# Third chunk of an attention layer: scores clipped in their PSUM bank, biases added from there

## The chip, the cores and the metric

The kernel runs on one core of a Trainium2 chip. The metric is the device time of one execution in microseconds (us). Engines: TensorE (PE; its weight loads are PEld), VectorE (DVE), ScalarE (ACT), GpSimd (POOL) and SyncE (SP), which here issues most DMA transfers. Each engine works through its own queue in order and waits on semaphores for the others. SBUF is the large on-chip memory; PSUM, in banks of 128 x 512 float32, is where TensorE puts its products.

## The reference

A chain of layers, each added to the residual stream x of shape 2 x 1024 x 256 (batch, sequence, features): an attention with ALiBi biases, a feed-forward network with ternary weights, a Mamba block and a gated feed-forward network that keeps two of each four activations. The change is in the attention: 16 heads of 128, and cut to what matters

```python
xn = layernorm(x)
q, k, v = xn @ Wq.T, xn @ Wk.T, xn @ Wv.T            # 16 heads x 128
s = q @ k.T / sqrt(128)                              # clipped to +-1024
s = s + slope[h] * arange(kv_len) + causal           # causal: -inf for later keys
x = x + softmax(s) @ v @ Wo.T
```

## The kernel before

**Chunks and heads.** The two sequences of 1024 rows are cut in two halves each, four chunks `CH[k] = (b, u)` of 512 queries. `attention()` goes through chunks and heads in order; per head it makes four query tiles `j` of 128 rows in `scores`. A tile's keys reach up to width `W = (u * 4 + j + 1) * 128`: in the chunks with `u = 0` (the first and the third, k = 0 and 2) W is 128, 256, 384 and 512, in the others 640 to 1024.

**One tile.** A score product (`s`, L362) goes into one of the two PSUM banks of tag "s". It is the negated score. DVE's clip (L366, scalar_tensor_tensor) takes the minimum with `CLIP` and the maximum with `lower`, a constant SBUF tile which is −1024 or, for masked keys, a huge number, and writes the SBUF tile `ss`. DVE's reduce (L372, tensor_tensor_reduce) adds the head's biases `alibi` from SBUF in place and accumulates the minimum `nm`; ACT's exponential (L377) uses `nm` as its bias and accumulates the row sum `rs`. Two tiles later (`LAG`) `turn` transposes the tile (`pt` on PE L293, copy `pT` L296), then `values` makes `z` (L304, copy `zs` L309), and `project` makes `o` (L318) and adds it to x, scaled by the reciprocal `rr` (L314, L324). The next head's `pq`, `pk` (L335) and `pv` (L342) are issued in the middle of a head.

**What runs beside it.** While chunk k's attention runs, `rest(k - 1)` brings the chunk before through its other three layers. A table of costs (`cost`) spreads these pieces between the attention's tiles. A tile scheduler orders each engine's instructions from modelled times when the program is built, and chooses the engine of every `nc.any` copy; so an edit of one place can move others. Beside the third chunk (k = 2) these stand, for the second chunk: the ternary FFN (`g_f`, `u_f` L441, `ssp` L491, `fo` L502), the Mamba block's projections (`in` L608, `dtl`, `bcp`), its scan, and the kept-two FFN.

**The scan.** The Mamba block has 512 channels in four blocks c of 128, and 16 states n. For every (c, n): SP's DMA fetches the rows `bs` and `cs`; POOL multiplies `db = du * bs` (L736); ACT makes `da = exp(dl * a)` into PSUM (L750); DVE scans `hs` (L757); POOL multiplies `hc = hs * cs` (L771); PE adds `hc` transposed into the bank `y` (L701). Each block needs `dl` and `du` first: `dt` (PE L547), four activations, `sr` (DVE L568, L569), `dl` (POOL L570, and DVE L572 beside the third chunk) and `du` (POOL L574). These steps of block c + 1 are issued at n = 8 of block c. `db` and `hs` have four buffers each, `hc` five, `cs` four and `bs` five. After a block's 16 states, `gate` copies `y` out, turns it back and multiplies it by the gate `sz` (L793).

**Banks.** PSUM has eight banks, shared by tags: "s" 2, "mm" 3 (turns, z, o, q, k, v), "y" 1, "r" 2 (FFN, Mamba, `da`).

Of the kernel before, what the change touches and what calls it, by code (L numbers as in the profile page):

```python
# [18 lines left out]
B, S, D = 2, 1024, 256  # L19
# [15 lines left out]
CLIP = 1024.0  # L35
# [6 lines left out]
def kernel(  # L42
# [190 lines left out]
    for h in range(H):  # L233
        nc.gpsimd.affine_select(
            out=slope, in_=slope, compare_op=ALU.not_equal, fill=-SLOPES[h], base=-h,
# [18 lines left out]
    lower = ac.tile([P, S], F32, name="lower")  # L254
    nc.gpsimd.memset(lower, -CLIP)
    nc.gpsimd.affine_select(
        out=lower[:, S - P :], in_=lower[:, S - P :], compare_op=ALU.is_ge,
# [97 lines left out]
    def scores(k, h, j, st):  # L355

        W = (CH[k][1] * UT + j + 1) * P
        s = a3.tile([P, S], F32, tag="s", name=f"ss_{k}_{h}_{j}", bufs=4)
        for k0 in range(0, W, 512):
            n = min(512, W - k0)  # L360
            sp = ps_s(f"s_{k}_{h}_{j}_{k0}")
            nc.tensor.matmul(  # L362
                sp[:, :n], lhsT=st["qT"][:, j * P : (j + 1) * P], rhs=st["kT"][:, k0 : k0 + n],
                start=True, stop=True,
            )
            nc.vector.scalar_tensor_tensor(  # L366
                s[:, k0 : k0 + n], sp[:, :n], CLIP, lower[:, S - W + k0 : S - W + k0 + n],
                op0=ALU.min, op1=ALU.max,
            )
        nm = a3.tile([P, 1], F32, tag="nm", name=f"nm_{k}_{h}_{j}")  # L370
        pace["front"] = tiles[-2] if len(tiles) >= 2 else None
        pace["tile"] = nc.vector.tensor_tensor_reduce(  # L372
            out=s[:, :W], in0=s[:, :W], in1=st["alibi"][:, :W], scale=1.0,
            scalar=3.0e38, op0=ALU.add, op1=ALU.min, accum_out=nm,
        )
        tiles.append(pace["tile"])
        nc.scalar.activation(  # L377
            s[:, :W], s[:, :W], AF.Exp, bias=nm, scale=-1.0, accum_out=st["rs"][:, j : j + 1]
        )
        return s  # L380

    def attention():
# [7 lines left out]
        for i, (k, h) in enumerate(heads):  # L390
# [8 lines left out]
            for j in range(UT):  # L399
                s = scores(k, h, j, st)  # L400
                later.append((LAG, lambda a=(k, h, j, s, st): turn(*a)))
                if j == UT - 1:
                    later.append((LAG, lambda a=(k, h, st): values(*a)))
                    later.append((LAG + 1, lambda a=(k, h, st): project(*a)))
                if j == UT - 1 and h == H - 1:
                    for _, f in later:
                        f()
                    later = []
                else:
                    now = [f for n, f in later if n == 0]  # L410
                    later = [(n - 1, f) for n, f in later if n]
                    for f in now:
                        f()
                if j == 1 and i + 1 < len(heads):
                    qkv(*heads[i + 1], live[0], xns[heads[i + 1][0]])
                if j == 0 and h == H - 1 and k + 1 < len(CH):

                    with tc.issue_after(tiles[-UT].ins) if k == 0 else nullcontext():
                        normed(k + 1)
                yield k  # L420
# [464 lines left out]
    def kept_two_ffn(k):  # L885

        b, u = CH[k]
        W = 2 * U
        with ExitStack() as gctx:
# [158 lines left out]
```

## Time and profile before

Three runs took 1833.47, 1836.29 and 1837.93 us.

| | us |
|---|---|
| median of the three runs | 1836.29 |
| profiled execution, span | 1836.9 |
| PE busy | 1718.3 (94%) |
| DVE busy | 1218.3 (66%) |
| ACT busy | 963.7 (52%) |
| POOL busy | 832.2 (45%) |

The profiled execution's own time is its span of 1836.9 us, 0.6 above the median: what is read in the trace is read against that span, and nothing to speak of lies around it. The third chunk's attention lies between about 733 and 1113 us of the span.

How to read the lines shown below: a group of instructions has its line of the code, engine and operation, the tile it writes and the tiles it reads, shapes and count, then busy time and the mean of one in ns, then the engine's idle time just before them and what ended it. A row of windows gives a stretch of the span and each engine's busy time with its number of instructions, then TensorE's granted clock (1.00 is full speed), the DMA engines' share and GB/s. A row of the order in time gives start, duration, engine, line and operation.

### The profile page before, as it was taken

What the parts mean: (1) busy time and instruction counts of PE and PEld (TensorE: products, weight loads), DVE (VectorE), ACT (ScalarE), POOL (GpSimd) and SP (SyncE); (2) the same over time, 40 slices, a digit from 0 to 9 for tenths busy, and PEclk for the clock granted to TensorE, in tenths of its full rate; (3) what the DMA queues carried; (4) which work ended last, traced back from release to release, by engine and by line L of the source; (5) the groups of instructions that cost most, each with busy time, mean ns of one, the idle gap of its engine ahead of it and who ended that gap; (6) DMA issues with size and microseconds to landing.
All of it is one profiled execution on the core that took longest, in us unless ns stands there. A gap on an engine that the chain in (4) does not pass through costs nothing. (4 is left out here: it accounts for less than half of the span.)

```text
span 1836.9 us, 24217 instructions
## 1 busy us (share of the span) xinstructions
PE 1718.3 (94%) x7956; PEld 1144.2 (62%) x7956; DVE 1218.3 (66%) x2349; ACT 963.7 (52%) x1789; POOL 832.2 (45%) x674
## 2 busy tenths in 40 slices
PE   7999999998999999998888999999999999998899
PEld 4666666555656557755555667756656565566895
DVE  5666555777785473458886565557788655667975
ACT  3444474656563553555554545566555446446742
POOL 3324032588892000419998000418898500035870
PEclk9999999999999999999999999999999999999999
DMA  6443512466662311337787324227665430212541
GB/s 201 128 142 128 193 46 88 149 203 204 216 202 91 103 52 48 125 109 232 245 247 224 116 71 141 82 67 228 226 214 184 142 115 26 75 53 86 178 136 57
DMA packets 178301, 255.99 MB, mean 139 GB/s; under 512 B 16240, under 2 KB 90992, under 8 KB 177152
## 3 DMA queue, kind: packets, MB, share of 16 engines
q1 hardware_dynamic: 176752, 241.61, 41.4%
q0 software_dynamic: 1152, 12.58, 1.9%
q8 instruction: 63, 1.03, 0.2%
q14 instruction: 62, 0.51, 0.1%
q10 hardware_dynamic: 272, 0.26, 0.0%
HBM read 232.04 MB, written 22.35 MB: 138 GB/s over the span
## 5 line engine op out<-in xcount | busy, mean ns | idle before, releaser
L771 POOL TENSOR_TENSOR hc<-hs,cs 128x512 f32<-128x512 f32 x256 | 362.1, 1428 | 10.8 <-DVE ss L366 3.1
L362 PE MATMUL s<-kT,qT 128*128 128x512 f32 (+3 forms) x768 | 302.7, 495 | 19.9 <-DVE ss L366 18.0
L377 ACT ACTIVATE ss<-ss,nm 128x128 f32<-128x128 f32 (+7 forms) x256 | 198.8, 776 | 183.5 <-DVE nm L372 174.1
L366 DVE SCALAR_TENSOR_TENSOR ss<-s,lower 128x512 f32<-128x512 f32 (+3 forms) x384 | 204.6, 549 | 121.0 <-PE s L362 119.4
L736 POOL TENSOR_TENSOR db<-du,bs 128x512 f32<-128x512 f32 x192 | 259.2, 1356 | 44.4 <-DVE hs L757 30.6
L304 PE MATMUL z<-pT,v 128*128 128x512 f32 (+3 forms) x768 | 264.5, 492 | 10.9 <-ACT pT L296 10.2
L372 DVE CUSTOM_DVE_ANT_0 ss<-ss,alibi 128x128 f32<-128x128 f32 (+7 forms) x256 | 241.3, 945 | 3.5
L750 ACT ACTIVATE da<-dl,a_neg 128x512 f32<-128x512 f32 x256 | 177.9, 698 | 115.6 <-DVE hs L757 90.6
L304 PEld LDWEIGHTS z<-pT,v 128*128 128x128 f32 x768 | 142.8, 190 | 145.1 <-issue 92.7
L296 ACT COPY pT<-pt 128x512 f32<-128x512 f32 (+3 forms) x321 | 145.4, 474 | 162.0 <-PE pt L293 160.4
L293 PE MATMUL pt<-ident,ss 128*128 128x128 f32 x1152 | 180.3, 279 | 32.1 <-DVE x L324 18.5
L293 PEld LDWEIGHTS pt<-ident,ss 128*128 128x128 f32 x1152 | 140.0, 142 | 94.7 <-DVE x L324 33.0
L362 PEld LDWEIGHTS s<-kT,qT 128*128 128x128 f32 x768 | 127.9, 193 | 84.1 <-issue 43.4
L757 DVE TENSOR_TENSOR_SCAN hs<-da,db 128x512 f32<-128x512 f32 x128 | 153.8, 1210 | 38.6 <-ACT da L750 20.8
L757 DVE TENSOR_TENSOR_SCAN hs<-da,carry,db 128x512 f32<-128x512 f32 x128 | 159.1, 1269 | 24.4 <-POOL hc L771 14.7
L324 DVE SCALAR_TENSOR_TENSOR x<-o,rr,x 128x256 f32<-128x256 f32 x256 | 108.9, 476 | 76.7 <-PE o L318 76.5
L701 PE MATMUL y<-ident,hc 128*128 128x128 f32 x1024 | 144.8, 279 | 8.4 <-POOL hc L771 8.4
L342 PEld LDWEIGHTS pv<-wv,xT_a 128*128 128x128 f32 x1024 | 124.4, 192 | 37.1 <-issue 25.3
L342 PE MATMUL pv<-wv,xT_a 128*128 128x128 f32 x1024 | 125.8, 275 | 5.5 <-ACT zs L309 3.4
L701 PEld LDWEIGHTS y<-ident,hc 128*128 128x128 f32 x1024 | 121.0, 145 | 14.3 <-POOL hc L771 11.9
L318 PE MATMUL o<-wo,zs 128*128 128x256 f32 x512 | 125.4, 386 | 4.1 <-ACT kT L338 3.0
L335 PE MATMUL pq<-xT_a,wq 128*128 128x512 f32 x256 | 122.7, 601 | 0.7 <-ACT xT_a L148 0.7
(204 smaller groups left out, 2468.7 us busy)
## 6 DMA issues: line engine op xcount, KB each, us to landing
cs<-bcd SPq DMA_DIRECT2D x256, 256.0 KB, 3.8
bs<-bcd SPq DMA_DIRECT2D x192, 256.0 KB, 4.3
alibi<-alibi_d SPq DMA_DIRECT2D x32, 512.0 KB, 4.2
wq<-in_wqT_dram SPq DMA_DIRECT2D x64, 128.0 KB, 3.5
wk<-in_wkT_dram SPq DMA_DIRECT2D x64, 128.0 KB, 3.1
wv<-in_wvT_dram SPq DMA_DIRECT2D x64, 128.0 KB, 2.8
wo<-in_woT_dram SPq DMA_DIRECT2D x64, 128.0 KB, 2.8
alibi<-alibi_d SPq DMA_DIRECT2D x32, 256.0 KB, 3.6
```

What stands on the lines that cost most here:

```text
L293: nc.tensor.transpose(tp[:, i, :], s[:, (kb0 + i) * P : (kb0 + i + 1) * P], ident)
L304: nc.tensor.matmul(zp[:, q0:], lhsT=st["v_all"][:, kb, :], rhs=st["pts"][kb // 4][:, kb % 4, q0:], start=(kb == 0), stop=(kb == last),)
L342: nc.tensor.matmul(vp[:, t, :], lhsT=xT[:, c, t * P : (t + 1) * P], rhs=st["v"][:, c, :], start=(c == 0), stop=(c == KC - 1),)
L362: nc.tensor.matmul(sp[:, :n], lhsT=st["qT"][:, j * P : (j + 1) * P], rhs=st["kT"][:, k0 : k0 + n], start=True, stop=True,)
L366: nc.vector.scalar_tensor_tensor(s[:, k0 : k0 + n], sp[:, :n], CLIP, lower[:, S - W + k0 : S - W + k0 + n], op0=ALU.min, op1=ALU.max,)
L372: pace["tile"] = nc.vector.tensor_tensor_reduce(out=s[:, :W], in0=s[:, :W], in1=st["alibi"][:, :W], scale=1.0, scalar=3.0e38, op0=ALU.add, ...
L377: nc.scalar.activation(s[:, :W], s[:, :W], AF.Exp, bias=nm, scale=-1.0, accum_out=st["rs"][:, j : j + 1])
L701: nc.tensor.matmul(yTs[c][:, t * P : (t + 1) * P], lhsT=h[:, t * P : (t + 1) * P], rhs=ident, is_transpose=True, start=start and t == 0, s ...
L736: nc.gpsimd.tensor_tensor(db[i], du, brow.pop(i), ALU.mult)
L750: nc.scalar.activation(da[i], parts[c][0], AF.Exp, scale=a_neg[:, c, n : n + 1])
L757: nc.vector.tensor_tensor_scan(out=hs[i], data0=da.pop(i), data1=db.pop(i), initial=0.0 if first else carry[:, n, c : c + 1], op0=ALU.mult ...
L771: nc.gpsimd.tensor_tensor(hc[i], hs.pop(i), crow.pop(i), ALU.mult)
```

## The change

In the third chunk, where the whole tile fits one bank, the clip writes its result back into the PSUM bank it reads, and the reduce takes its first input from that bank and writes `ss` in SBUF for the first time. In the other chunks nothing changes (in the first one `k` is 0). The bank is thus read by the reduce, where it was last read by the clip. In the changed program the clip has line L368, the reduce L374 and the exponential L379; all lines behind are two higher.

```diff
         W = (CH[k][1] * UT + j + 1) * P
+        in_bank = k and W <= 512
         s = a3.tile([P, S], F32, tag="s", name=f"ss_{k}_{h}_{j}", bufs=4)
...
+            clipped = sp[:, :n] if in_bank else s[:, k0 : k0 + n]
             nc.vector.scalar_tensor_tensor(
-                s[:, k0 : k0 + n], sp[:, :n], CLIP, lower[:, S - W + k0 : S - W + k0 + n],
+                clipped, sp[:, :n], CLIP, lower[:, S - W + k0 : S - W + k0 + n],
                 op0=ALU.min, op1=ALU.max,
             )
...
         pace["tile"] = nc.vector.tensor_tensor_reduce(
-            out=s[:, :W], in0=s[:, :W], in1=st["alibi"][:, :W], scale=1.0,
+            out=s[:, :W], in0=clipped if in_bank else s[:, :W], in1=st["alibi"][:, :W], scale=1.0,
             scalar=3.0e38, op0=ALU.add, op1=ALU.min, accum_out=nm,
         )
```

## The prediction

> **What bounds the kernel now.** I first read the busy rows of the page: TensorE (PE) is the busiest engine over the whole span, with GpSimd (POOL) at under half.
>
> ```profile
> PE 1718.3 (94%) x7956; PEld 1144.2 (62%) x7956; DVE 1218.3 (66%) x2349; ACT 963.7 (52%) x1789; POOL 832.2 (45%) x674
> ```
>
> The edit touches only the third chunk's attention, so the average says little. Second view: the busy time in four stretches, chosen by what runs beside that attention (second chunk's ternary FFN, its Mamba input projection, its scan, its kept-two FFN).
>
> ```profile
> core 0: us, PE busy (x) PEld busy (x) DVE busy (x) ACT busy (x) POOL busy (x), PEclk, DMA share, GB/s
> 733.00:781.00 48.00, 45.77 (x238) 34.73 (x238) 23.57 (x68) 26.04 (x54) 22.03 (x19) 1.00 0.37 124
> 781.00:831.00 50.00, 48.44 (x176) 26.15 (x175) 31.48 (x69) 29.76 (x56) 11.17 (x13) 1.00 0.36 117
> 841.00:999.00 158.00, 125.90 (x644) 90.06 (x643) 131.75 (x189) 84.77 (x174) 156.37 (x120) 0.94 0.78 238
> 1000.00:1113.00 113.00, 111.25 (x468) 72.87 (x467) 59.08 (x142) 50.92 (x98) 5.61 (x5) 1.00 0.31 102
> ```
>
> PE is the bound in three of them (97 to 98% busy, whole clock). In the scan stretch (841 to 999) it isn't: POOL is busy for 156.37 of 158 us. There POOL sets the end, and VectorE (DVE) and PE have time to spare. Third view: the groups by shape, first in the scan stretch and then in the stretch behind it, where POOL is nearly idle.
>
> ```profile
> L372 DVE CUSTOM_DVE_ANT_0 ss<-ss,alibi 128x384 f32<-128x384 f32 x7 | 8.5, 1207 | 0.0
> L372 DVE CUSTOM_DVE_ANT_0 ss<-ss,alibi 128x512 f32<-128x512 f32 x7 | 7.3, 1049 | 0.2
> L366 DVE SCALAR_TENSOR_TENSOR ss<-s,lower 128x512 f32<-128x512 f32 x6 | 4.0, 672 | 0.0
> L366 DVE SCALAR_TENSOR_TENSOR ss<-s,lower 128x384 f32<-128x384 f32 x6 | 3.2, 540 | 0.0
> ```
>
> ```profile
> L366 DVE SCALAR_TENSOR_TENSOR ss<-s,lower 128x512 f32<-128x512 f32 x5 | 3.4, 687 | 1.3 <-PE s L362 1.3
> L372 DVE CUSTOM_DVE_ANT_0 ss<-ss,alibi 128x512 f32<-128x512 f32 x4 | 2.8, 692 | 0.2
> L372 DVE CUSTOM_DVE_ANT_0 ss<-ss,alibi 128x384 f32<-128x384 f32 x5 | 2.8, 552 | 0.0
> ```
>
> The reduce (L372, two inputs in SBUF) goes from 552 to 1207 ns and from 692 to 1049 ns once POOL is busy; the clip (L366, one input in PSUM) doesn't stretch (687 and 672). Fourth view: the order in time of POOL and of DVE around one head, where the reduces of widths 256, 384 and 512 start at 883.14, 886.49 and 890.79.
>
> ```profile
> 883.40 1.45 POOL L736 TENSOR_TENSOR db<-du,bs 128x512 f32<-128x512 f32 x1
> 884.82 1.27 POOL L771 TENSOR_TENSOR hc<-hs,cs 128x512 f32<-128x512 f32 x1
> 887.28 1.58 POOL L771 TENSOR_TENSOR hc<-hs,cs 128x512 f32<-128x512 f32 x1
> 891.28 1.72 POOL L736 TENSOR_TENSOR db<-du,bs 128x512 f32<-128x512 f32 x1
> ```
>
> ```profile
> 883.14 0.59 DVE L372 CUSTOM_DVE_ANT_0 ss<-ss,alibi 128x256 f32<-128x256 f32 x1
> 886.49 1.24 DVE L372 CUSTOM_DVE_ANT_0 ss<-ss,alibi 128x384 f32<-128x384 f32 x1
> 890.79 1.07 DVE L372 CUSTOM_DVE_ANT_0 ss<-ss,alibi 128x512 f32<-128x512 f32 x1
> ```
>
> The POOL product that meets a reduce takes 1.45, 1.58 and 1.72 us, where others take 1.27: the two engines make each other wait. Beside a clip or a scan POOL stays at 1.27.
>
> **The change part by part.** Only the 64 tiles of the third chunk (16 heads, widths 128 to 512) change; no DMA and no arithmetic instruction is added. The profiled execution spans 1836.9 us, 0.6 above the median of the runs (1836.29), so I add changes to the median as they are.
>
> 1. *Collision of reduce and POOL product.* The reduce keeps one SBUF input (the biases) and so looks like the clip. Per head it costs POOL 0.06 (the width-128 tile: 1.32 against 1.26), 0.18, 0.32 and 0.45, together 1.01 us. Seven heads (27 tiles) lie in the scan stretch: 7.1 us. Assigned operation by operation in the trace it is 7.2. POOL runs without gaps there, so that is a gain on the path: **−7.2**. What collides besides (L569, L572, with two SBUF inputs, 2.2 us) stays. The reduce itself gets shorter too (25.5 us for 27 tiles there, 13.2 at the undisturbed durations), on an engine with time to spare: 0.
>
> 2. *Clip writes PSUM, reduce reads PSUM.* No row shows DVE writing PSUM. ScalarE does: its 128x512 exponential into PSUM (L750) takes 691 ns, the one into SBUF (L377) 724: by that the clip would even be 0.03 us shorter. From the other side, a second full pass over each width would be 0.53 us per 512 elements, 1.33 per head, 9.3 in the scan stretch, where DVE stands at 131.75 of 158 and loses 12.3 of stretched reduces. I take 0, by the nearest rows; even the dear end hides beside POOL. [...] Here the clip from PSUM (687) is no slower than the reduce from SBUF (692), so I price it at nothing.
>
> 3. *Bank held until the reduce is done.* The two "s" banks came free after the clip; now a score product waits for the reduce two tiles back. Behind it on PE's queue stand z, the next head's q, k, v and the turns. The rows for this wait were PEld s on L366 at 31.3 us and PE s on L366 at 18.0 in the whole kernel. Beside the ternary FFN, where PE is the bound and two heads run, I take two or three of eight tiles as waiting for one reduce more (0.29 to 0.69 us, its undisturbed durations, mean 0.49): **+1.0** (0.5 to 1.5; a longer hold can't bring a gain). In the other stretches the wait shows in the order of work, steps 4 to 6. [...]
>
> 4. *Order around the projection.* In the built order, ScalarE loads tables three more times around the last gates (1.283 us each by the L377 table-load row), and a score product and transposes come ahead of dtl on PE (about 1.5 us). So the first db is some 2.7 us late; but the POOL order in time shows waits of 1.19 and 0.70 us for bs at 835.5 and 838.7, which this swallows: **+1.0** (0 to 2.7).
>
> 5. *The dt step at the two channel-block borders.* This is the largest loss. In the new order the score product of head 6, tile 3 stands behind the y additions of hc 0 to 4 (block 1), and z, q, k, v and dt (block 2) stand behind it. Before, z started at 885.0, with hc 3 and 4 still to come. POOL ends hc 4 at T = 888.86. So PE now waits until T, then 0.86 (the score products), 7.6 (z, pq, pk, pv), 1.8 (o) and the rest to dt: dt ends at about T + 12.0, against T + 7.4 before. The activations and both sr behind dt took 3.6 us: dl can start at T + 15.6. POOL gets there after ten products of 1.27, at T + 12.7, and waits **+2.9**; before, dl started at 902.19 with no gap. The same at the next border (head 8): there POOL already waits 0.69 at 947.78, and by the same count it becomes **+2.2** more. The first border keeps its order.
>
> 6. *Ends.* The last block's y additions and heads 11 to 15 (slacks of 0.15 to 0.3 us used up): **+0.8**.
>
> 7. *Clock.* TensorE's clock drops to 0.50 for 3.4 us right after PE gaps (at 831.6, 858.9, 903.3, 923.8, 992.1). Step 5 makes two new gaps of about 2 us. One new drop at full load costs up to 1.7; none or two are possible: **+1.7** (0 to 3.4).
>
> Sum: −7.2 + 1.0 + 1.0 + 2.9 + 2.2 + 0.8 + 1.7 = +2.4, so 1836.3 + 2.4 = 1838.7; I say 1839.
>
> **The rivals.**
>
> *A, forecast: collision gone, its gain paid back at the dt borders.* With the small ends of 3, 4 and 7 it is −0.8, with the large ones +6.3: 1835.5 to 1842.5. For it: at both borders POOL has no slack. Against: the order is static, but where PE waits depends on when POOL finishes, and POOL now finishes sooner.
>
> *B, faster: the gain stays.* If dt's chain is shorter than I count (the z matmuls start before T), POOL gets to dl with nothing late: with the small ends of 3, 4 and 7 that is −7.2 + 0.5 + 0.8 = −5.9; without one of the five clock drops as well −7.6. So 1828.7 to 1830.4; I take 1829.5. It needs dt to end before T + 9. For it: POOL is at 99% in that stretch and every product is counted.
>
> *C, slower: PE falls five products behind.* hc has five buffers, a db and an hc take 2.5 us, so POOL can run 12.6 us ahead of the y additions. The stretch of PE without y additions behind the held score product is some 10 us by the rows. If a waiting score product and a slow clock take it beyond 12.6, POOL stops at hc at three heads (5, 7 and 9's z) for some 3 us each: +2.4 + 9 = +11.4, about 1848. Against it: 2.6 us are missing.
>
> *D: the change doesn't separate the engines,* as the write of ss and the biases are still in SBUF. Then the 7.2 stays lost while the reordering is paid: +9.6, 1846. Against it: the clip, with lower and ss in SBUF, doesn't collide.
>
> **How the numbers follow.** A 0.40, B 0.28, C 0.24, D 0.08. About 0.3% (5.5 us) is what a measurement here can tell from no change: faster means under 1830.8, slower over 1841.8. A gives 0.30 same, 0.07 slower, 0.03 faster; B 0.25 faster, 0.03 same; C 0.24 slower; D 0.07 slower, 0.01 same. Together faster 0.28, same 0.34, slower 0.38. The range takes in B with a further 1.2 us and C with a further 2: 1827.5 to 1850. A's own is 1835.5 to 1842.5.
>
> **What would show it.** Step 1: products L771 and L736 average about 1.28 in the scan stretch, and the reduces there fall to about 290, 420, 555 and 690 ns; if they stay at 1.0 to 1.2 us, D. Step 2: the clip stays at 687 ns for 512; near 1.2 us would be the dear end. Step 5: POOL waits of 2 to 3 us for sr at its second and third L570; none means B. Step 7: more 0.5 digits around these. C: idle time of L771 released by PE's y. The forecast is wrong if POOL's scan stretch shrinks by 7 us with nothing behind it, or grows.

## The result, and the profile after

The changed kernel takes 1848.88 us (median of 4 runs, 1846.68 to 1850.38), the kernel before 1837.11 in the runs beside it: a ratio of 1.006, with a 95% interval of 1.0043 to 1.0078. It is slower by some 11 us. Executions of one and the same program lie up to 16 us apart in the runs below, so the ratios with their intervals decide there, and a single trace only says where the time went.

The first two views are the busy row of the page and the same four stretches as before. The busy totals of DVE and POOL fell (1218.3 to 1206.8 and 832.2 to 823.4), and the span rose by 8.0 us, to 1844.9.

```profile
PE 1722.6 (93%) x7956; PEld 1146.4 (62%) x7956; DVE 1206.8 (65%) x2351; ACT 965.1 (52%) x1790; POOL 823.4 (45%) x674
```

```profile
733.00:781.00 48.00, 45.42 (x223) 34.19 (x222) 23.03 (x66) 26.84 (x56) 21.58 (x19) 0.96 0.36 120
781.00:831.00 50.00, 49.55 (x183) 26.92 (x181) 27.00 (x61) 27.83 (x48) 6.65 (x9) 1.00 0.30 102
841.00:999.00 158.00, 126.96 (x604) 88.32 (x603) 118.73 (x183) 83.51 (x171) 142.39 (x115) 0.89 0.73 231
1000.00:1113.00 113.00, 107.74 (x461) 70.11 (x460) 61.90 (x147) 52.34 (x101) 13.62 (x12) 1.00 0.34 109
```

In the scan stretch POOL is no longer back to back: busy 142.39 of 158 us, where it was 156.37. It did five operations fewer in the same time. TensorE's granted clock there fell from 0.94 to 0.89.

The groups by shape in the scan stretch (taken from 845 to 1010, as all of it is later) show that the change did what it says:

```profile
L773 POOL TENSOR_TENSOR hc<-hs,cs 128x512 f32<-128x512 f32 x58 | 74.6, 1290 | 2.6 <-PE y L703 1.8 <-DMA cs<-bcd 0.9
L738 POOL TENSOR_TENSOR db<-du,bs 128x512 f32<-128x512 f32 x56 | 71.3, 1275 | 11.9 <-DMA cs<-bcd 4.6 <-DVE hs L759 4.5 <-DMA bs<-bcd 2.8
L368 DVE SCALAR_TENSOR_TENSOR s<-s,lower 128x512 f32<-128x512 f32 x7 | 4.9, 693 | 4.1 <-PE s L363 3.9
L374 DVE CUSTOM_DVE_ANT_0 ss<-s,alibi 128x512 f32<-128x512 f32 x7 | 4.8, 683 | 0.2
L374 DVE CUSTOM_DVE_ANT_0 ss<-s,alibi 128x384 f32<-128x384 f32 x7 | 3.8, 539 | 0.1
```

The reduce takes 683 and 539 ns beside a busy POOL, where it took 1049 and 1207. The products hc and db fell from 1346 and 1362 ns to 1290 and 1275: 58 x 56 ns + 56 x 87 ns = 8.1 us of POOL time. But idle time of 2.6 and 11.9 us now stands ahead of these products. The order in time on POOL names it; the bracket is the wait before the operation:

```profile
856.56 1.27 POOL L572 TENSOR_TENSOR dl<-dl,sr 128x512 f32<-128x512 f32 x1 [1.42 <-DVE sr L571]
881.27 1.27 POOL L738 TENSOR_TENSOR db<-du,bs 128x512 f32<-128x512 f32 x1 [0.93 <-DMA bs<-bcd]
906.50 1.28 POOL L738 TENSOR_TENSOR db<-du,bs 128x512 f32<-128x512 f32 x1 [4.50 <-DVE hs L759]
909.87 1.27 POOL L572 TENSOR_TENSOR dl<-dl,sr 128x512 f32<-128x512 f32 x1 [0.69 <-DVE sr L571]
954.20 1.28 POOL L738 TENSOR_TENSOR db<-du,bs 128x512 f32<-128x512 f32 x1 [4.59 <-DMA cs<-bcd]
957.58 1.26 POOL L572 TENSOR_TENSOR dl<-dl,sr 128x512 f32<-128x512 f32 x1 [0.69 <-DVE sr L571]
991.58 1.26 POOL L738 TENSOR_TENSOR db<-du,bs 128x512 f32<-128x512 f32 x1 [1.60 <-DMA bs<-bcd]
1007.13 4.96 POOL L773 TENSOR_TENSOR hc<-hs,cs 128x512 f32<-128x512 f32 x4 [1.77 <-PE y L703]
```

The two large stops, 4.50 and 4.59 us, are at the second and third border between channel blocks. (The second one is put down to the transfer that came last by the profile; DVE stands still there as at the first.) The order in time on DVE and then on PE at the second border shows how it comes about:

```profile
895.11 0.70 DVE L368 SCALAR_TENSOR_TENSOR s<-s,lower 128x512 f32<-128x512 f32 x1 [1.59 <-PE s L363]
898.73 0.18 DVE L314 RECIPROCAL rr<-rs 128x4 f32<-128x4 f32 x1 [2.19 <-ACT ss L379]
903.49 1.74 DVE L324 SCALAR_TENSOR_TENSOR x<-o,rr,x 128x256 f32<-128x256 f32 x4 [4.58 <-PE o L318]
905.15 1.27 DVE L759 TENSOR_TENSOR_SCAN hs<-da,carry,db 128x512 f32<-128x512 f32 x1
907.14 0.92 DVE L570 TENSOR_SCALAR sr<-se 128x512 f32<-128x512 f32 x1 [0.20 <-ACT se L563]
```

```profile
889.80 0.66 PE L703 MATMUL y<-ident,hc 128*128 128x128 f32 x4 [1.80 <-POOL hc L773]
892.25 1.11 PE L703 MATMUL y<-ident,hc 128*128 128x128 f32 x4 [1.79 <-POOL hc L773]
893.15 1.92 PE L363 MATMUL s<-kT,qT 128*128 128x512 f32 x2
894.86 2.50 PE L304 MATMUL z<-pT,v 128*128 128x512 f32 x8
902.42 1.89 PE L318 MATMUL o<-wo,zs 128*128 128x256 f32 x8
904.26 1.02 PE L549 MATMUL dt<-dtls,dt_sb 128*128 128x512 f32 x2
```

PE waits for hc 3 and hc 4 before it gets to the score product and z, then runs q, k, v and o. DVE stands at x, which waits for o, with the scan behind it; POOL has no free db buffer left and stands too. The late dt holds POOL as well: sr (L570) waits for ScalarE's work on dt, and POOL's dl (L572, 909.87) waits for sr (L571).

Where the lateness grows, against the kernel before (positive is later; the first row is noise from ahead of the change):

| work, in order of time | before, us | shift in the changed kernel |
|---|---|---|
| last gate and up product of the first chunk's kept-two FFN | 668.32 | −1.76 |
| last fo product beside heads 0 and 1 | 780.79 | +1.42 |
| last in product | 808.39 | +0.95 |
| first db | 824.43 | +4.50 |
| seventh db | 835.49 | +3.65 |
| eighth db | 838.69 | +2.92 |
| db ahead of the second border | 891.28 | +3.32 |
| db behind it | 907.84 | +7.38 |
| db ahead of the third border | 936.56 | +5.67 |
| db behind it | 949.00 | +9.80 |
| last db but one | 991.07 | +10.58 |
| the same of the second chunk | 1076.55 | +10.77 |

So some 4.7 us (−1.76 to +2.92) are lost ahead of the scan's steady part, which begins behind the eighth db, and 7.7 in it, although POOL's products became 8 us shorter there.

### The profile page after: what moved, and what is told of

Read it like the earlier page. It is cut to its first block, busy times and chain, and to the rows that moved or that the text cites. A ratio compares the mean times of both kernels' runs of the same rounds, so it can differ in the third digit from the quotient of the medians.

```text
span 1844.9 us, 24222 instructions
## 1 busy us (share of the span) xinstructions
PE 1722.6 (93%) x7956; PEld 1146.4 (62%) x7956; DVE 1206.8 (65%) x2351; ACT 965.1 (52%) x1790; POOL 823.4 (45%) x674
## 5 line engine op out<-in xcount | busy, mean ns | idle before, releaser
L379 ACT ACTIVATE ss<-ss,nm 128x128 f32<-128x128 f32 (+7 forms) x256 | 198.3, 775 | 163.1 <-DVE nm L374 151.5
L738 POOL TENSOR_TENSOR db<-du,bs 128x512 f32<-128x512 f32 x192 | 251.0, 1313 | 55.3 <-DVE hs L759 38.7
L368 DVE SCALAR_TENSOR_TENSOR ss<-s,lower 128x512 f32<-128x512 f32 (+2 forms) x320 | 174.0, 561 | 97.0 <-PE s L363 95.6
L374 DVE CUSTOM_DVE_ANT_0 ss<-ss,alibi 128x640 f32<-128x640 f32 (+1 forms) x192 | 193.6, 1010 | 4.3 <-DMA alibi<-alibi_d 1.7
```

The lines of the kernel that those rows point to most:

```text
L368: nc.vector.scalar_tensor_tensor(clipped, sp[:, :n], CLIP, lower[:, S - W + k0 : S - W + k0 + n], op0=ALU.min, op1=ALU.max,)
L374: pace["tile"] = nc.vector.tensor_tensor_reduce(out=s[:, :W], in0=clipped if in_bank else s[:, :W], in1=st["alibi"][:, :W], scale=1.0, sca ...
L379: nc.scalar.activation(s[:, :W], s[:, :W], AF.Exp, bias=nm, scale=-1.0, accum_out=st["rs"][:, j : j + 1])
L738: nc.gpsimd.tensor_tensor(db[i], du, brow.pop(i), ALU.mult)
```

## Experiments

**All widths but 256, or only 256.** The score product of tile 3 takes the bank of tile 1. Is it that one held bank which moves the order?

```diff
-        in_bank = k and W <= 512
+        in_bank = k and W <= 512 and W != 256      # first run
+        in_bank = k and W == 256                   # second run
```

> Clip and reduce stay in the bank for the third chunk's widths 128, 384 and 512; the width-256 tile takes the way through SBUF again. The score product of tile 3 needs the bank of tile 1 (width 256), so it is no longer held back, and the built order of PE around the channel-block borders is that of the kernel before (z and dt with hc 2 and 3 still to come). Theory 1 (the order: the gain of POOL is eaten at the borders, where x waits for o on DVE): the collision gain is 0.06 + 0.32 + 0.45 = 0.83 us per head, 5.8 over seven heads, the two 4.5 us stops of POOL go, and the time is 1830 to 1833. Theory 2 (any bank held until the reduce costs, as PE waits in its queue): three of four banks are still held, so most of the loss stays, 1843 or more. Theory 3 (the operations on PSUM themselves are dear): 1843 or more, with longer clips or reduces.

> Only the width-256 tile of the third chunk is clipped and reduced in the bank. Theory 1 (order): PE's order has z of heads 5, 7 and 9 behind one to two more y additions than before, and the score product of tile 3 behind hc 4, so the borders cost some 2 to 4 us each, while the collision gain is only 0.18 per head, 1.3 in all: 1839 to 1844. Theory 2 (every held bank costs about a quarter): +2 to +3 over the kernel before, less 1.3: about 1838.

All but 256: 1840.51 against 1838.68, ratio 0.9999 (0.9984 to 1.0013). Only 256: 1844.14, ratio 1.0032 (1.0020 to 1.0044), +5.9 us. The width-256 tile alone brings more than half of the loss, the amount that theory 1 gives, and three held banks of four cost no more than they gain, which speaks against theories 2 and 3. But the place is not the one that theory 1 names. In the trace of the second run POOL's stops for scans and sr at the second and third border are only 1.1 to 1.3 us each, and the shift, counted as in the table, is +2.65 at the eighth db, +3.06 at the last db but one and +7.09 at the second chunk's last gate and up product: this loss lies ahead of the scan and behind it.

The expected gain of 5.8 us came in a part of the first run's executions only. Five of the twelve took 1829.7 to 1835.8 us, on average 5.2 below the mean of the kernel before, at a mean granted clock of 0.987 to 0.989; the other seven took 1840.4 to 1843.9 at 0.985 or 0.986. By the means, 1838.15 against 1838.45, nothing is left of it. The kept trace is of one of the five. So in this program the time goes with the clock; which of the two moves the other is not shown.

**The late score product without a held bank.**

```diff
+            with tc.issue_after(ended["y"].ins) if k == 2 and j == 3 and h in (6, 8, 10) else nullcontext():
               nc.tensor.matmul(
                 sp[:, :n], lhsT=st["qT"][:, j * P : (j + 1) * P], rhs=st["kT"][:, k0 : k0 + n],
```

> The kernel before (every tile through SBUF, banks free after the clip), with the score product of tile 3 of heads 6, 8 and 10 issued behind the last y addition that stood ahead of it in the program: PE's order at the borders becomes that of the run with only width 256 in the bank. No bank is held and nothing else changes. Theory 1 (order alone does it): slower than the kernel before by 2 to 7 us, 1839 to 1844, with POOL stops at the borders. Theory 2 (the held bank does it): within 1 us of the kernel before.

1841.41, ratio 1.0015 (1.0007 to 1.0024), +2.8 us: the order costs time without any held bank. Not where it was expected, though: POOL's stops at the borders are 1.30 us, the shift of the last db but one is 0.9 us smaller than that of the first (−1.5 and −0.6), and the loss appears behind the scan (the Mamba output's first product is 4.5 us late). In this order z waits for hc 3 only, not hc 4.

**Only the heads outside the scan stretch, and only those in it.**

```diff
+        in_bank = k and W <= 512 and not 4 <= h <= 10      # first run
+        in_bank = k and W <= 512 and 4 <= h <= 10          # second run
```

> In the bank only for the third chunk's heads 0 to 3 and 11 to 15, outside the scan stretch; heads 4 to 10 go through SBUF. No collision with POOL's scan products to gain from, and the order at the last three borders is that of before. It prices what the held banks cost beside the ternary FFN, the projections (a later first db: the changed kernel was 3.65 us late there) and the kept-two FFN. Theory 1: +2 to +4 us, 1838 to 1841, from the later start of the scan alone. Theory 2: the held banks of nine heads cost in proportion, +5 or more.

> All four widths in the bank, but only for the third chunk's heads 4 to 10, those beside the scan; the other nine heads go through SBUF. Theory 1 (start and borders each lose): the first db starts as in the kernel before (no 3 to 6 us of late start), the two POOL stops of about 4.5 us at the second and third border stay, and the collision gain is -8 as in the changed kernel; the scan stretch alone was 6 us longer there, so +4 to +7 against the kernel before. Theory 2 (the late start makes the borders collide, nothing else): with the start restored the gain stays and the time is 5 or more below.

Outside: 1843.86, ratio 1.0024 (1.0014 to 1.0034), +4.4 us, though the order at the three borders is that of before. In its trace the first db is 6.8 us late. Inside: 1844.12, ratio 1.0035 (1.0022 to 1.0048), +6.4 us. In its trace the first db is 1.3 us later than the shift ahead of the change (+1.66 against +0.37), and POOL's two stops are there:

```profile
902.38 1.28 POOL L738 TENSOR_TENSOR db<-du,bs 128x512 f32<-128x512 f32 x1 [4.36 <-DVE hs L759]
950.22 1.28 POOL L738 TENSOR_TENSOR db<-du,bs 128x512 f32<-128x512 f32 x1 [4.71 <-DVE hs L759]
```

4.4 + 6.4 = 10.8, against 11.0 for all heads (0.6%): within their intervals the two losses are separate and add up. Theory 2 of the second run, that only the late start makes the borders collide, falls.

**The collision gain by itself.** With widths 384 and 512 of heads 4 to 10, the built order of PE and POOL is that of the kernel before; with 128 as well it differs by one swap on PE.

```diff
+        in_bank = k and 384 <= W <= 512 and 4 <= h <= 10               # first run
+        in_bank = k and W <= 512 and W != 256 and 4 <= h <= 10         # second run
```

> In the bank only the widths 384 and 512 of heads 4 to 10. The built order of PE and POOL is that of the kernel before, ACT's and SP's differ by one swap each, DVE's scans move around a few clips. So this is the collision gain alone: (0.32 + 0.45) x 7 = 5.4 us of POOL time. Theory 1 (POOL bounds the scan stretch; only the order loses): -4 to -5.5. Theory 4 (POOL is only one of two bounds there: PE's chain of z, o and dt at the borders ends almost as late, so POOL waits for DVE or PE instead): about half, -1 to -3, with new POOL stops behind scans.

> In the bank the widths 128, 384 and 512 of heads 4 to 10; the order of PE is that of the kernel before but for one swap. Against the run with all heads but width 256 it leaves out the other nine heads, which started the scan 1.4 us later. Theory 1: the gain of 5.8 us (0.83 x 7) with little lost, -4 to -6. Theory 4: half of it, -1 to -3.

First: 1836.84 against 1838.43, ratio 0.9995 (0.9984 to 1.0007). Second: 1841.10, ratio 1.0012 (0.9998 to 1.0025). Neither is faster: theory 4 is the nearer for the first, whose interval, −2.9 to +1.3 us, takes in no gain at all, and the second is slower than either theory had it. The traces show one reason. The same eight z products of head 8 on PE, the second run ahead of the first:

```profile
930.88 4.63 PE L304 MATMUL z<-pT,v 128*128 128x512 f32 x8 [2.73 <-ACT pT L296]
```

```profile
928.77 2.42 PE L304 MATMUL z<-pT,v 128*128 128x512 f32 x8 [0.25 <-ACT pT L296]
```

After a wait of 2.73 us they run at half the granted clock (0.50 from 930.2 for 6.8 us in the windows, so from within the wait on), and POOL then waits 2.92 us for y and 1.76 for hs. Without the wait they run at the full one. That the wait set off the drop is the author's reading of these two traces, not tried.

**Which operand collides.** In the kernel before, the reduce of width 512 of heads 4 to 10 keeps two SBUF inputs and writes the bank instead:

```diff
-            out=s[:, :W], in0=s[:, :W], in1=st["alibi"][:, :W], scale=1.0,
+            out=sp[:, :W] if out_bank else s[:, :W], in0=s[:, :W], in1=st["alibi"][:, :W], scale=1.0,
...
-            s[:, :W], s[:, :W], AF.Exp, bias=nm, scale=-1.0, accum_out=st["rs"][:, j : j + 1]
+            s[:, :W], sp[:, :W] if out_bank else s[:, :W], AF.Exp, bias=nm, scale=-1.0, accum_out=st["rs"][:, j : j + 1]
```

> The kernel before, with the reduce of width 512 of heads 4 to 10 still reading two SBUF inputs (clipped scores and biases) but writing its sum into the PSUM bank, from where the exponential reads it. It tells which operand makes reduce and POOL product wait for each other. If it is the second SBUF input: the reduce stays stretched (about 1.0 us against 0.69) and the POOL products that meet it stay at 1.72. If it is the SBUF output: both go to 0.69 and 1.27. The time is expected 0 to 5 us above the kernel before, as the bank is held until the exponential.

One run, 1840.84. The groups from 841 to 1000:

```profile
L373 DVE CUSTOM_DVE_ANT_0 s<-ss,alibi 128x512 f32<-128x512 f32 x7 | 8.5, 1212 | 0.1
L772 POOL TENSOR_TENSOR hc<-hs,cs 128x512 f32<-128x512 f32 x59 | 79.0, 1343 | 0.3 <-DVE hs L758 0.3
```

The reduce stays stretched (1212 ns), and POOL's products stay as they were before (hc 1343 ns here, 1346 before; db 1354 and 1362, though some of these meet reduces of other widths). In the changed kernel the reduce of the same width, with one SBUF input and its output in SBUF, takes 683. So here the second SBUF input is enough to collide, without an SBUF output.

**What is POOL time worth in this stretch?** Eight hc products of the kernel before, shortened to 128 columns or done twice:

```diff
+                w = P if k == 1 and n in (4, 12) else U                          # first run, hc over :w
+                for _ in range(2 if k == 1 and n in (4, 12) else 1):             # second run, hc repeated
```

> The kernel before, untouched in its attention; in the second chunk's scan the products hc of states 4 and 12 of each block multiply 128 of 512 columns only (the y additions read those four times; this leaves out part of the computation). The order of PE, DVE, ACT and SP is that of the kernel before. Eight POOL operations become about 0.9 us shorter: 7 us less POOL work, the size of the collision gain, with no bank held and no other engine touched. If POOL alone sets the end of the scan stretch (the prediction's step 1): -6 to -7 us. If PE's chain at the borders ends almost as late (theory 4): -1 to -3, as in the run with widths 384 and 512.

> The kernel before with the same eight products hc done twice: eight more POOL operations of 1.23 us, start to start, 9.8 us. If POOL sets the end, +9 to +10. If it is as often PE that is late, less: +5 to +8. Against the run with less POOL work it shows whether the price is the same in both directions.

Less: 1834.28 against 1838.11, ratio 0.9976 (0.9961 to 0.9990), −4.4 us, where the eight products became 6.6 us shorter (533 ns each, against 1363 for the others). More: 1846.48, ratio 1.0036 (1.0022 to 1.0051), +6.6 of 9.8. In both directions about two thirds of POOL's time reaches the end, by the middle values; the intervals (1.8 to 7.2 and 4.0 to 9.4) allow from a quarter to all of it. The clock was not the same in the two: in the kept traces it stood at half for 10.2 us with less POOL work and for 23.9 with more, so a part of the first gain may be PE's.

**DVE's wait at x.**

```diff
-            for i in range(2):
+            for i in range(0 if k == 2 and h in (5, 7, 9) else 2):
                 xt = x[k][:, t + i, :]
```

> All widths of heads 4 to 10 in the bank, as in the run of that name (which took 1844 with POOL stops of 4.4 and 4.7 us at the second and third border), without the additions of o to x for heads 5, 7 and 9 (left out of the computation: 12 DVE operations of 0.4 us). PE's order stays. Theory 1 (DVE stands at x, waiting for o, with the scans behind it): the stops shrink from 4.4 and 4.7 to 1 to 3 us (sr still follows the late dt), and the time falls by 3 to 6, to 1838 to 1841. If the late dt alone makes them, they stay above 3.5 and the time falls by less than 2.

> The control of it: the kernel before without the same twelve additions. Neither border has a stop of DVE at x that POOL waits for, so the time stays within 2 us of the kernel before.

On the scan-heads run: 1842.50, ratio 1.0023 (1.0008 to 1.0038), +4.2 where it was +6.4. On the kernel before: 1835.73, ratio 0.9989 (0.9979 to 0.9999), −2.0. The difference of the two is 6.2, where it was 6.4: taking out x did nothing for the borders, and POOL's stops stayed at 4.49 and 4.26 us. DVE's order in time says why:

```profile
892.19 0.18 DVE L314 RECIPROCAL rr<-rs 128x4 f32<-128x4 f32 x1 [2.58 <-ACT ss L379]
897.92 0.29 DVE L296 COPY pT<-pt 128x128 f32<-128x128 f32 x1 [5.55 <-PE pt L293]
898.35 1.28 DVE L759 TENSOR_TENSOR_SCAN hs<-da,carry,db 128x512 f32<-128x512 f32 x1
```

The rebuilt order put a pT copy where x had stood. It waits for a transposition that stands behind o on PE, so DVE's scans were blocked as long. That x in particular is to blame is thus refuted. The run's other theory, that the late dt alone makes the stops, has its condition met (both above 3.5 us), and dl starts 4.4 us after dt's end here (898.74 to 903.09). That any instruction waiting for PE's late chain ahead of the scan blocks it agrees with the traces too, but no run with none such there, or with an early dt, was made.

The stops do not decide the time by themselves either. The kept trace of the scan-heads run without x has both of them and is of its shortest execution (1836.55), while the trace with only width 256 in the bank has stops of 1.1 to 1.3 us at an execution of 1845.75.

## Why the prediction was right or wrong

The range held the time; the number did not. 1839 was 10 us low, and the likeliest case, a gain just paid back, did not come about. The range reached up to 1850 only for rival C, whose mechanism did not occur, so that it held the time was luck.

- **Step 1, the collision: right in size, wrong in worth.** 7.2 us of POOL time were forecast, 8.1 measured. But it was entered in full as "a gain on the path". The runs with less and more POOL work give about two thirds, and the run with the order unchanged (widths 384 and 512) shows −0.9 us with an interval of −2.9 to +1.3 for 5.4 us of collisions.
- **Step 2, the price on PSUM: right.** The clip into PSUM takes 693 ns beside the scan and 694 behind it (672 and 687 into SBUF), the reduce out of it 683 and 689 (692 undisturbed from SBUF). The dear end, 0.53 us more for 512 columns (the clips' 672 − 540 ns for 128 columns, four times), shows nowhere in these rows.
- **Steps 3 and 4, the start: 2.0 forecast, 4.7 in the trace; +4.4 in the run without the scan heads.** The waits for banks of step 3 are negligible (0.5 us on PEld s between 733 and 781, where it was 0.9). PE ran at half clock (0.50) for 3.4 us from 775.8 beside the fo products instead; that the change caused this drop is not shown. Step 4 was too small: dtl started 2.7 us later on PE as counted, but the first db 4.5 later. The two waits for bs, which were to swallow 1.9, gave back 1.6 (+4.50 to +2.92 at the eighth db).
- **Step 5, the borders: the place was right, the size not.** Forecast +2.9 and +2.2 at the second and third; measured 4.50 + 0.69 and 4.59 + 0.69 − 0.69, together 9.8. PE's lateness was nearly as counted: T is 892.19 in the new trace, dt ends at T + 13.1 (forecast 12.0) and dl starts at T + 17.7 (15.6). The step that failed is the way from dt to dl, entered with 3.6 us as read from the kernel before. Its rows say more:

```profile
895.26 1.02 PE L547 MATMUL dt<-dtls,dt_sb 128*128 128x512 f32 x2
899.55 1.55 DVE L569 TENSOR_TENSOR sr<-se,sr 128x512 f32<-128x512 f32 x1
```

From dt's end (896.28) to sr's end (901.10) that is 4.8 us, and 4.6 were measured in the changed kernel (905.28 to 909.87). dt itself came 1.1 later than counted: ahead of z stand the y additions of hc 4, which the sum did not name, and the clock was at 0.50 there (from 891.8 for 3.4 us). With dl at T + 17.7 against T + 12.7 the wait is 5.0 instead of 2.9, nearly the whole of the 5.19 measured. POOL in fact stopped before dl, at T + 9.8, at a db whose buffer waits for a scan that stands on DVE behind an instruction waiting for PE. The working left this second hold-up out, but by these numbers it adds little: dl alone would have stopped POOL almost as long.

- **Step 6:** the smaller stops (1.4 at the first border, 1.9 for bs and cs near 884, 1.8 in the last block, 1.8 for y) were 0.8 in the sum; the kernel before has two at the end, 1.1 and 1.6 for cs. The first border was priced at nothing since z and dt keep their places there; the stop came all the same.
- **Step 7, the clock: mis-sized.** One new drop of 3.4 us was entered (1.7). Between 733 and 1115 the clock stood at half for 23.9 us before and 41.0 after (counted in windows of 0.4 us); that is up to 8.5 us of PE work, half of the difference. Two of the five drops that step 7 lists, at 903.3 and 992.1, had lasted 6.8 us and not 3.4, and the last began within a gap of PE (3.72 us, to 993.40), not behind it. All four executions of the changed kernel have a mean granted clock of 0.984 or 0.985, the 80 of the kernel before in the experiments 0.983 to 0.992, on average 0.989. No run holds the order and changes the clock, so how much of the 11 us comes by the clock and how much by the waits stays open.
- **The rivals.** C named 1848, but its mechanism, PE five products behind, is 1.77 us in the trace: a right number for a wrong reason. B failed on its own condition, dt before T + 9. D is refuted by the groups.

## What to carry to other kernels

Here a buffer held longer was paid for in the order that the scheduler made of it (+2.8 us for the late score product without a held bank), not in the wait for the buffer (0.5 us on PEld s between 733 and 781): compare the built orders, and follow a late instruction on every engine that has something waiting for it, not only along the chain one has in mind. Time taken off POOL, 99% busy in its stretch, or put on it reached the end only in part here (−4.4 us of 6.6, +6.6 of 9.8, by the middle values); shortening and lengthening a few of an engine's operations measures it. And where a change has several parts, the part that moves the order (here one tile width of four) can be left out: that took the loss away here (ratio 0.9999), though on average no gain was left.

## What the runs showed of the hardware

DVE's clip of 128x512, reading and writing one PSUM bank in place, took 693 ns beside the scan and 694 behind it, where the same clip into SBUF had taken 672 and 687. Two traces with the same PE order around the z products of head 8 differ by a wait of 2.5 us ahead of them and then by nearly a factor of two in their time (4.63 and 2.42 us); that the wait is the cause is not shown. Between 733 and 1115 the clock stood at half for 23.9 us in the trace before and for 41.0 in the changed kernel's, with 7956 PE products in each trace.
